# Two causal attention layers in half-height bands on TensorE, with the future zeroed after the exponential

## The chip, the core and the metric

One core of a Trainium2 chip runs the whole kernel. The metric is the device time of one execution in microseconds; lower is better. The time before is the median of three runs.

## The reference

A decoder of four blocks on x of 8 batches x 256 positions x 128 channels. Each block has self-attention, cross-attention to a context of 512 positions, and a feed-forward part, each behind a layer norm and added to x. The change touches the two causal layers of the last block, L3_attn and L3_xattn: 16 heads of 8 channels, 256 queries and 256 keys, every query seeing only keys up to its own position. L3_xattn also masks keys by batch and multiplies its result by a gate.

```python
# L3_attn
scores = jnp.einsum('bhid,bhjd->bhij', Qh, Kh) / jnp.sqrt(jnp.asarray(Dh, dtype=x.dtype))
causal = jnp.tril(jnp.ones((S, S), dtype=x.dtype))
scores = scores * causal - NEG_BIG * (1.0 - causal)
attn = jax.nn.softmax(scores, axis=-1)
vals = jnp.einsum('bhij,bhjd->bhid', attn, Vh)
...
# L3_xattn
scores = jnp.where(mask[:, None, None, :] == 0, neg_inf, scores)
future = jnp.triu(jnp.ones((Sq, Sk), dtype=bool), k=1)
scores = jnp.where(future[None, None, :, :], neg_inf, scores)
attn = jax.nn.softmax(scores, axis=-1)
attn = jnp.nan_to_num(attn, nan=0.0)
context = jnp.einsum('bhqk,bhkd->bhqd', attn, v)
gate = jax.nn.sigmoid(query @ Wg.T + bg)
output = gate * context @ Wo.T
```

## The kernel before, in words

**Order.** The layers run one after the other, with some work of the layer before (a "guest": the tail of L2_ffn in L3_attn) stepped in between. TensorE's instructions keep the order in which the program is written; on the other engines and on the queues that issue transfers, the scheduler sets the order. Every queue runs in order.

**The two causal layers** are both `_heads_attention(causal=True)`, one loop over t = 0 to 127 (batch b = t // 16, head h = t % 16) and some steps behind it. One step does:

- `maxima(t)` (line 510): the scores of head t, queries as rows, in two products of 128 and 256 keys into a PSUM tile `mh_sps` (the upper right quarter is left out); VectorE adds the causal bias, takes the maximum and stores its negative in `mh_nm` (line 523, two instructions a head).
- every fourth step, `turn` (line 544): GpSimd splits the four heads' maxima into a rounded part and the rest (`mh_hi`, `mh_nx`, lines 549 to 552); two steps later `turned` (line 554): TensorE turns them over (`mh_mps`), ScalarE copies them to `mh_m`, and one transfer that ScalarE issues (line 563) writes them into rows 96 and 97 of `q`.
- `exps(t - 12)` (line 565): first a product that writes the causal bias into the PSUM tile `mh_bsps` (256 wide in L3_attn; 384 wide in L3_xattn, with the key mask), then two products that add the scores with keys as rows. Rows 96 and 97 of `k` are ones, so the products subtract the maximum at the same time. ScalarE takes the exponential of the 384 columns (line 583, `mh_e`).
- every fourth step, `combine` (line 614) for the four heads just finished: 8 products with the values, each into a strip of 32 columns (`mh_ops`), f32 and so run in two passes, 16 in the trace. The values have a column of ones, which gives the sums. ScalarE copies the result (`mh_osb`); later `divide`, `finish`, `project_out` and `normed` end the batch.

**q and k** of the next batch are made in steps 2 to 10: TensorE projects, ScalarE adds the bias (`mh_kf`, `mh_qf`), GpSimd splits each into a rounded part and the rest (`mh_kp`, `mh_qp`, lines 428 and 429; a product of two such sums is made in one pass from four parts), and SP issues the transfers that spread heads over rows: 4 for k (line 434) and 8 for q (line 439). A head pair shares 64 rows of k: 32 rows belong to the even head and 32 to the odd one. q has one slot for each of 16 heads, with zeros in the 32 rows of the other head, so products have 96 rows (maxima) or 128 rows (exps, with the maxima's rows and zeros).

**What stands ready.** `third` (line 377), called in L2_ffn, makes a third buffer for q (four copies on ScalarE) and a transposed causal bias. `_l3_masks` (line 792), called in the middle of L3_attn, loads the key mask broadcast to 128 rows, turns it into a bias on VectorE, and gives `key_bias` (line 811), in which GpSimd adds causal and key bias with four instructions a batch.

Of the kernel before, what the change touches and what calls it, by code (L numbers as in the profile page):

```python
# [46 lines left out]
TOP = 96  # L47
FLOOR = -1.0e20
# [118 lines left out]
def _pack(inputs):  # L167
# [3 lines left out]
    for layer, mats in w.items():  # L171
# [8 lines left out]
    arrays["key_mask"] = np.ascontiguousarray(np.asarray(inputs["mask_BxS2_ik0"])[:, :S]).reshape(1, B * S)  # L180
    arrays["key_mask_t"] = np.ascontiguousarray(
        np.asarray(inputs["mask_BxS2_ik0"])[:, :S].reshape(B, 2, P).transpose(2, 0, 1)
    ).reshape(P, 2 * B)
# [161 lines left out]
class _Heads:  # L345
# [5 lines left out]
    def __init__(self, E, ctx):  # L351
# [10 lines left out]
        self.made = 0  # L362
# [14 lines left out]
    def third(self, ctx):  # L377

        pool = ctx.enter_context(self.E.tc.tile_pool(name="hd3", bufs=1, side="right"))
        q = pool.tile([P, H, S], F32R, name="mh_q2")  # L380
        for i in range(0, H, 4):
            self.E.nc.scalar.copy(
                q[:, i : i + 4, :].rearrange("p h n -> p (h n)"), self.E.plain[:, 0:1].to_broadcast([P, 4 * S])
            )
        self.q.insert(0, q)

        t = self.E.causal_t = pool.tile([P, 3, P], F32, name="causal_t")
        self.E.nc.gpsimd.memset(t, 0.0)
        for i in (0, 2):
            self.E.nc.gpsimd.affine_select(  # L390
                out=t[:, i, :], in_=t[:, i, :], compare_op=ALU.is_ge, fill=NEG, base=0,
                pattern=[[1, P]], channel_multiplier=-1,
            )

    def begin(self, layer, keys, bias=True):

        E, nc, W = self.E, self.E.nc, self.E.w(layer)
        self.layer, self.keys, self.bias = layer, keys, bias
# [11 lines left out]
    def steps(self, b):  # L410
# [29 lines left out]

        def values():
            ps = self.g.tile([P, n // P, D], F32, tag="g", name="mh_vps")
            for c in range(n // P):
                self.mm(ps[:, c, :], self.keys(b)[:, c * P : c * P + P], W("wv"), start=True, stop=True)
            to = v[:, :, : H * VW].rearrange("p k (h d) -> p k h d", d=VW)
            nc.scalar.copy(to[:, :, :, :DH], ps.rearrange("p k (h d) -> p k h d", d=DH))
# [6 lines left out]
        two = lambda f, g: lambda: (f(), g())  # L453
        spread = [lambda j=j: spread_k(j) for j in range(4)]
        spread += [lambda r=r, j=j: spread_q(r, j) for j in range(4) for r in range(2)]
        early = [lambda: project("k", self.keys(b), n), lambda: project("q", E.xt(b), S), rest]
        return early, [two(*spread[i : i + 2]) for i in range(0, 12, 2)], values
# [20 lines left out]
def _heads_attention(E, ctx, causal=False, mask=None, key_bias=None, gate=False, guest=None, known=(0,), pace=None):  # L478
# [10 lines left out]
    lag = 12 if causal else 8  # L489
# [4 lines left out]
    pe = pool("mhe", 8 if causal else 10)  # L494
# [13 lines left out]
    units, extras = {}, {}  # L508

    def maxima(t):  # L510

        b, h = divmod(t, H)
        if h == 0 and key_bias:
            extras[b] = key_bias(b)
        if h % 4 == 0:
            u = units[t // 4] = SimpleNamespace(r=ready[b], es={}, extra=extras.get(b))
            u.nm = sm.tile([P, 2, 4], F32, name="mh_nm")
        u = units[t // 4]
        q, k = u.r.q[:TOP, h, :], u.r.k[:TOP, h // 2, :]
        def lowest(at, scores, lowered):  # L520

            rest = wk.tile([P, S if causal else n], BF16, name="mh_rest")
            nc.vector.tensor_tensor_reduce(  # L523
                rest[:, : scores.shape[1]], scores, lowered, -1.0, -FLOOR, ALU.add, ALU.min, accum_out=at
            )

        col = slice(h % 4, h % 4 + 1)
        if causal:
            ps = ps_a.tile([P, 3 * P], F32, tag="a", name="mh_sps")
            mm(ps[:, :P], q[:, :P], k[:, :P], start=True, stop=True, skip_group_check=True)  # L530
            mm(ps[:, P:], q[:, P:], k, start=True, stop=True, skip_group_check=True)
            by = (u.extra or E.causal)[0].rearrange("p i k -> p (i k)")
            lowest(u.nm[:, 0, col], ps[:, :P], by[:, :P])
            lowest(u.nm[:, 1, col], ps[:, P:], by[:, P:])
            return
        for c in range(2):
            ps = ps_a.tile([P, n], F32, tag="a", name="mh_sps")
            mm(ps, q[:, c * P : c * P + P], k, start=True, stop=True, skip_group_check=True)
# [5 lines left out]
    def turn(i):  # L544

        u = units[i]
        nm = u.nm
        hi = sm.tile([P, 2, 4], F32R, name="mh_hi")
        nc.gpsimd.tensor_copy(hi, nm)  # L549
        u.nx = sm.tile([P, 2, 2, 4], F32, name="mh_nx")  # L550
        nc.gpsimd.tensor_copy(u.nx[:, :, 0, :], hi)
        nc.gpsimd.tensor_tensor(u.nx[:, :, 1, :], nm, hi, ALU.subtract)  # L552

    def turned(i):

        u = units[i]
        ps = pg.tile([P, 2, P], F32, tag="g", name="mh_mps")
        for c in range(2):
            turn_over(ps[:8, c, :], u.nx[:, c, :, :].rearrange("p a h -> p (a h)"))
        m = wk.tile([8, S], F32R, name="mh_m")  # L560
        nc.scalar.copy(m, ps[:8].rearrange("p c q -> p (c q)"))  # L561
        h0 = 4 * (i % 4)
        nc.scalar.dma_start(u.r.q[TOP : TOP + 2, h0 : h0 + 4, :].bitcast(F32), m.bitcast(F32))

    def exps(t):

        u, h = units[t // 4], t % H
        if causal:
            ps = ps_b.tile([P, 384], F32, tag="b", name="mh_bsps")
            if u.extra:  # L570
                mm(ps, E.ident16, u.extra[1], start=True, stop=False, skip_group_check=True)
            else:
                mm(
                    ps.rearrange("p (i q) -> p i q", q=P)[:, 0:3:2, :], E.later,
                    E.ident16.unsqueeze(1).to_broadcast([P, 2, P]), start=True, stop=False, skip_group_check=True,
                )
# [752 lines left out]
def _l2_ffn(E, ctx):  # L1329
# [31 lines left out]
    if E.heads:  # L1361
        E.third()
# [419 lines left out]
```

## Time and profile before

| | us |
|---|---|
| median of three runs | 1775.19 (1772.72 to 1775.53) |
| span of the profiled execution | 1770.2 |
| of it before the first scores of L3_attn | 1339 |
| L3_attn, 1339 to 1528 | 189; TensorE busy 161.4, VectorE 112.4, ScalarE 101.3, GpSimd 68.9 |
| L3_xattn, 1528 to 1707 | 179; TensorE busy 160.7, VectorE 114.2, ScalarE 97.4, GpSimd 70.9 |
| L3_ffn, from 1707 | 63 |

The profile is one execution. PE is TensorE's products, PEld its loads of the stationary operand, DVE is VectorE, ACT ScalarE, POOL GpSimd; a q behind an engine's name, or SPq, is a queue that issues transfers. A line of a window shows its start and end, its length, the busy time of each engine with the number of instructions in brackets, TensorE's granted clock, and the share and rate of the transfers. A line of a group shows the source line, engine, operation, tile written and tiles read, shapes and number, with durations as minimum, median and maximum in ns. In a timeline a line shows start and length in us and how many instructions of a kind were merged; brackets hold the idle time ahead of it and what ended it.

### The profile page before, as it was taken

The numbers are of one execution on the slowest core, as the hardware profiler recorded it, in microseconds if no ns is written. First come the engines' busy times: TensorE is split into PE (matmuls) and PEld (weight loads), VectorE is DVE, ScalarE is ACT, GpSimd is POOL, SyncE is SP. The second block draws the span as 40 slices with busy tenths as digits, with TensorE's granted clock in tenths as the row PEclk, the third lists the DMA queues.
The fourth block names the chain that finished last, engine by engine and source line by source line (L and its number), as shares of the span: only waits on it lengthen the run. The fifth ranks groups of instructions, "written<-read, shape, count | busy, mean of one in ns | idle before, by whom it ended". The sixth has DMA issues, their size and how long they took to land. (4 is left out here: it accounts for less than half of the span.)

```text
span 1770.2 us, 29308 instructions
## 1 busy us (share of the span) xinstructions
PE 1462.7 (83%) x10103; PEld 1055.3 (60%) x10141; DVE 1148.5 (65%) x3857; ACT 881.5 (50%) x1830; POOL 495.7 (28%) x987
## 2 busy tenths in 40 slices
PE   5689989999999998785578888878946799799986
PEld 3457677766665555453446666656615677677763
DVE  4567666765636676777667777767465666466756
ACT  7245455555652344325535655557644466355543
POOL 3122222221110122223433433332113433244422
PEclk9799999999999999997979999989956899899998
DMA  4011011104100000000111101111002221122100
GB/s 154 13 37 36 6 34 37 36 11 155 38 1 1 1 1 1 0 1 1 36 35 36 28 14 37 37 37 45 2 10 65 85 69 38 50 55 59 39 1 25
DMA packets 47236, 60.43 MB, mean 34 GB/s; under 512 B 5232, under 2 KB 36976, under 8 KB 46448
## 3 DMA queue, kind: packets, MB, share of 16 engines
q1 hardware_dynamic: 44720, 56.99, 11.9%
q8 instruction: 80, 1.31, 0.3%
q10 hardware_dynamic: 2368, 1.57, 0.3%
q14 instruction: 68, 0.56, 0.1%
HBM read 14.50 MB, written 1.05 MB: 9 GB/s over the span
## 5 line engine op out<-in xcount | busy, mean ns | idle before, releaser
L460 PE MATMUL mh_sps<-mh_k,mh_q 96*128 96x512 f32 (+2 forms) x1024 | 323.4, 398 | 49.0 <-DMA mh_q<-mh_qp 16.9
L460 PE MATMUL mh_bsps<-mh_q,mh_k 128*128 128x256 f32 (+1 forms) x1536 | 352.7, 335 | 7.6 <-ACT mh_e L596 4.1
L596 ACT ACTIVATE mh_e<-mh_bsps 128x512 f32<-128x512 f32 x512 | 281.0, 599 | 117.6 <-PE mh_bsps L460 110.4
L460 PEld LDWEIGHTS mh_bsps<-mh_q,mh_k 128*128 128x128 f32 x1536 | 265.8, 198 | 32.6 <-issue 6.9
L460 PEld LDWEIGHTS mh_sps<-mh_k,mh_q 96*128 96x128 f32 x1024 | 172.5, 202 | 96.2 <-issue 35.9
L523 DVE CUSTOM_DVE_ANT_0 mh_rest<-mh_sps,mask_b 128x512 bf16<-128x512 f32 x256 | 167.2, 685 | 81.4 <-PE mh_sps L460 78.4
L460 PE MATMUL mh_ops<-mh_e,mh_v 128*32 128x256 f32 (+1 forms) x3072 | 194.0, 373 | 1.3 <-DVE mh_nm L523 0.8
L542 DVE TENSOR_REDUCE mh_nm<-mh_sps 128x1 f32<-128x512 f32 x256 | 165.0, 680 | 25.7 <-PE mh_sps L460 25.2
L583 ACT ACTIVATE mh_e<-mh_bsps 128x384 f32<-128x384 f32 x256 | 118.6, 494 | 57.8 <-PE mh_bsps L460 33.5
L460 PEld LDWEIGHTS mh_ops<-mh_e,mh_v 128*32 128x32 f32 x3072 | 94.5, 111 | 66.1 <-ACT mh_e L583 5.8
L197 POOL TENSOR_SCALAR ln_rstd<-ln_mv 128x2 f32<-128x2 f32 x96 | 22.0, 229 | 386.4 <-DVE ln_mv L195 386.1
L549 POOL CAST mh_hi<-mh_nm 128x8 fp32r<-128x8 f32 x128 | 25.0, 195 | 337.9 <-DVE mh_nm L523 211.4
L523 DVE CUSTOM_DVE_ANT_0 mh_rest<-mh_sps,causal 128x128 bf16<-128x128 f32 (+1 forms) x256 | 79.4, 352 | 51.0 <-PE mh_sps L460 49.0
L523 DVE CUSTOM_DVE_ANT_0 mh_rest<-mh_sps,km_q 128x128 bf16<-128x128 f32 (+1 forms) x256 | 79.4, 350 | 43.8 <-PE mh_sps L460 42.5
L561 ACT CAST mh_m<-mh_mps 8x256 fp32r<-8x256 f32 x128 | 46.2, 361 | 102.1 <-PE mh_mps L463 100.2
L215 ACT COPY xt<-ln_ps 128x256 f32<-128x256 f32 x96 | 36.0, 375 | 120.5 <-PE ln_ps L463 62.3
L629 ACT COPY mh_osb<-mh_ops 128x256 f32<-128x256 f32 x128 | 47.7, 372 | 83.5 <-PE mh_ops L460 83.3
L886 ACT ACTIVATE moe_si<-moe_gps 128x512 f32<-128x512 f32 x64 | 38.0, 597 | 102.5 <-PE moe_gps L884 87.6
L460 PE MATMUL mh_bsps<-mask_t,ident 128*128 128x512 bf16 x219 | 84.7, 387 | 0.4 <-ACT mh_e L596 0.4
L201 DVE TENSOR_SCALAR ln_z<-x,ln_mv,ln_rstd 128x128 f32<-128x128 f32 x136 | 43.4, 360 | 54.9 <-POOL ln_rstd L198 54.7
L884 PE MATMUL moe_ups<-xt,w_L_ffn 128*128 128x512 f32 x128 | 69.2, 623 | 6.9 <-ACT moe_si L886 4.8
L463 PE MATMUL mh_mps<-ident,mh_nx 128*8 128x128 f32 x256 | 51.1, 282 | 27.7 <-POOL mh_nx L552 23.2
(360 smaller groups left out, 3086.8 us busy)
## 6 DMA issues: line engine op xcount, KB each, us to landing
mh_k<-mh_kp SPq DMA_DIRECT2D x64, 256.0 KB
mh_q<-mh_qp SPq DMA_DIRECT2D x256, 64.0 KB
mh_k<-mh_kp SPq DMA_DIRECT2D x64, 128.0 KB
w_L_ffn<-in_w_L_ffn SPq DMA_DIRECT2D x2, 1558.0 KB
w_L_attn<-in_w_L_attn SPq DMA_DIRECT2D x2, 1056.0 KB
ctx_t<-in_ctx_t SPq DMA_DIRECT2D x4, 512.0 KB
mh_q<-mh_m ACTq DMA_DIRECT2D x128, 8.0 KB
w_L_ffn<-in_w_L_ffn SPq DMA_DIRECT2D x2, 687.0 KB
```

The lines of the kernel that those rows point to most:

```text
L201: (engine or nc.vector).tensor_scalar(z[:, q, :], E.x[:, 2 * b + q, :], mv[:, q, 0:1], rstd[:, q : q + 1], ALU.subtract, ALU.mult)
L215: E.nc.scalar.copy(E.xt(b), ps.rearrange("p q t -> p (q t)"))
L460: return self.E.tc.keep_in_program_order(self.E.nc.tensor.matmul(*a, **kw))
L463: return self.E.tc.keep_in_program_order(self.E.nc.tensor.transpose(*a))
L523: nc.vector.tensor_tensor_reduce(rest[:, : scores.shape[1]], scores, lowered, -1.0, -FLOOR, ALU.add, ALU.min, accum_out=at)
L542: nc.vector.tensor_reduce(u.nm[:, c, col], ps, AX.X, ALU.max, negate=True)
L561: nc.scalar.copy(m, ps[:8].rearrange("p c q -> p (c q)"))
L583: nc.scalar.activation(e, ps, AF.Exp, scale=scale)
L596: nc.scalar.activation(e, ps, AF.Exp, scale=scale)
L629: nc.scalar.copy(osbs[b][:, u4 % 2, :], ops)
L884: nc.tensor.matmul(ps, W("w13")[:, o : o + P], xt, start=True, stop=True)
L886: nc.scalar.activation(si, pgate, AF.Silu)
```

## The change

In the causal layers even heads are put in rows 0 to 63 and odd heads in rows 64 to 127 of both q and k. In each band 32 rows hold the four parts of 8 channels, row 32 of q is ones and of k holds the key mask (or zero), the rows up to 61 are zero, and rows 62 and 63 hold the maxima in q and ones in k. Zeros and ones are written once, by 12 transfers of SP (`strips`). q needs only 8 slots for 16 heads, so that two tiles give four buffers; the third buffer is dropped. k takes 8 transfers in place of 4.

The products of `maxima(t)` and `exps(t - 13)` are written in turns, one of each; the lag is odd, so that they are of opposite bands. The bias product is dropped: the exponential is taken of all 384 columns and GpSimd then sets the future to zero in the two diagonal blocks. The key mask enters as a row of k, by two transfers a batch. `turned` comes three steps behind `turn` instead of two, its result is written by two transfers of SP instead of one of ScalarE, and `combine` comes two steps later. Ahead of the turning over and ahead of the value sums stands a filling product, a bf16 128 x 128 by 256 product into the PSUM tile that the following products overwrite.

```diff
+    def strips(self):
+        q0, q1 = self.q
+        half = H // 2
+        self.q = [q[:, at : at + half, :] for q in (q0, q1) for at in (0, half)]
+        for k in self.k:
+            self.rows(k, HIDE, LAST - HIDE, 0)
+            self.rows(k, LAST, 2, 1)
+        for q in (q0, q1):
+            self.rows(q, HIDE, 1, 1)
...
+        def strip(to, what, parts, r, j):
+            rows = slice(STRIP * r, STRIP * r + HIDE)
+            to = to[rows, :, :].bitcast(F32).rearrange("(d j) s n -> j d s n", j=4)
+            nc.sync.dma_start(to[j], got[what][64 * r : 64 * r + 64, parts[j], :])
+
+        def lower_k():
+            src = self.key_bias[b : b + 1, :]
+            for r in range(2):
+                at = STRIP * r + HIDE
+                nc.sync.dma_start(
+                    k[at : at + 1, :, :].bitcast(F32), src.unsqueeze(1).to_broadcast([1, H // 2, n])
+                )
...
+        ks = [lambda r=r, j=j: strip(k, "k", (0, 1, 0, 1), r, j) for j in range(4) for r in range(2)]
+        qs = [lambda r=r, j=j: strip(q, "q", (0, 0, 1, 1), r, j) for j in range(4) for r in range(2)]
+        if self.key_bias is not None:
+            ks.append(lower_k)
...
-    lag = 12 if causal else 8
+    lag = 13 if causal else 8
-    pe = pool("mhe", 8 if causal else 10)
+    pe = pool("mhe", 10 if causal else 10)
...
+    def warm(ps, times):
+        for _ in range(times):
+            mm(ps, E.ident16, E.causal[:, 0:2, :], **go)
...
         if causal:
+            rows = slice(STRIP * (h % 2), STRIP * (h % 2) + LAST)
+            q, k = u.r.q[rows, h // 2, :], u.r.k[rows, h // 2, :]
             ps = ps_a.tile([P, 3 * P], F32, tag="a", name="mh_sps")
-            mm(ps[:, :P], q[:, :P], k[:, :P], start=True, stop=True, skip_group_check=True)
-            mm(ps[:, P:], q[:, P:], k, start=True, stop=True, skip_group_check=True)
+            yield mm(ps[:, :P], q[:, :P], k[:, :P], **go)
+            mm(ps[:, P:], q[:, P:], k, **go)
...
     def turned(i):
+        if causal:
+            warm(ps, 1)
...
+        if causal:
+            for r in range(2):
+                at = STRIP * r + LAST
+                to = u.r.q[at : at + 2, 2 * (i % 4) : 2 * (i % 4) + 2, :]
+                nc.sync.dma_start(to.bitcast(F32), m[4 * r : 4 * r + 4, :].bitcast(F32))
+            return
         nc.scalar.dma_start(u.r.q[TOP : TOP + 2, h0 : h0 + 4, :].bitcast(F32), m.bitcast(F32))
...
     def exps(t):
-            if u.extra:
-                mm(ps, E.ident16, u.extra[1], start=True, stop=False, skip_group_check=True)
-            else:
-                mm(
-                    ps.rearrange("p (i q) -> p i q", q=P)[:, 0:3:2, :], E.later,
-                    E.ident16.unsqueeze(1).to_broadcast([P, 2, P]), start=True, stop=False, skip_group_check=True,
-                )
+            rows = slice(STRIP * (h % 2), STRIP * (h % 2) + STRIP)
+            q, k = u.r.q[rows, h // 2, :], u.r.k[rows, h // 2, :]
             for kt in range(2):
-                mm(
-                    ps[:, 256 * kt : 256 + P * kt], u.r.k[:, h // 2, kt * P : kt * P + P],
-                    u.r.q[:, h, kt * P :], start=False, stop=kt == 1, skip_group_check=True,
-                )
+                yield mm(ps[:, 256 * kt : 256 + P * kt], k[:, kt * P : kt * P + P], q[:, kt * P :], **go)
+            e = pe.tile([P, 3, P], F32, tag="e", name="mh_e")
+            flat = e.rearrange("p i q -> p (i q)")
+            nc.scalar.activation(flat, ps, AF.Exp, scale=scale)
+            own = e[:, 0:3:2, :]
+            nc.gpsimd.affine_select(
+                out=own, in_=own, compare_op=ALU.is_ge, fill=0.0, base=0, pattern=[[0, 2], [1, P]],
+                channel_multiplier=-1,
+            )
...
     def combine(i):
+        if causal:
+            warm(ops.rearrange("p (c q) -> p c q", q=P), 1)
...
+    def by_turns(s, e):
+        left = object()
+        while left is not None:
+            left = next(s, None)
+            left = next(e, None) or left
...
-        if t % 4 == 1 and 4 < t < H * B + 2:
+        if t % 4 == (2 if causal else 1) and 4 < t < H * B + 3:
             turned(t // 4 - 1)
...
-        c = t - lag - 4
+        c = t - lag - 4 - 2 * causal
```

`_l3_masks` loads the mask as 8 x 256 and makes one bias tile of it with one VectorE instruction on 8 rows; `key_bias`, `third` and the transposed bias are gone.

## The prediction

> **What bounds the kernel now.** The change touches the two causal layers alone, so I read their steady stretches first. The view of windows says how busy each engine is, and the exponentials (line 583, one for each head) say how long a batch of 16 heads takes. Each window below holds 16 of them and one cut by the edge.
>
> ```profile
> core 0: us, PE busy (x) PEld busy (x) DVE busy (x) ACT busy (x) POOL busy (x), PEclk, DMA share, GB/s
> 1447.40:1466.60 19.20, 17.93 (x182) 14.87 (x176) 11.83 (x76) 11.73 (x30) 6.81 (x21) 1.00 0.21 58
> 1581.60:1602.70 21.10, 19.06 (x183) 15.74 (x186) 13.94 (x81) 12.13 (x31) 10.06 (x26) 1.00 0.19 53
> ```
>
> ```profile
> 1447.40:1466.60 19.20, 7.29 (x17) 1.00 0.21 58
> 1581.60:1602.70 21.10, 7.49 (x17) 1.00 0.19 53
> ```
>
> A batch takes 19.2 us in L3_attn and 21.1 in L3_xattn, and TensorE is busy for 17.9 and 19.1 of it; no other engine passes 14. So TensorE sets the pace, with 1.3 and 2.0 us per batch in which it waits. What it does in one step (a head's scores for the maximum, mh_sps, and an older head's bias product and transposed scores, mh_bsps) shows in the timeline:
>
> ```profile
> 1446.14 0.10 PEld L460 LDWEIGHTS <-causal 128*128 128x128 bf16 x1
> 1446.15 0.32 PEld L460 LDWEIGHTS mh_bsps<-mh_q,mh_k 128*128 128x128 f32 x2
> 1446.39 0.30 PEld L460 LDWEIGHTS mh_sps<-mh_k,mh_q 96*128 96x128 f32 x2
> 1446.73 0.10 PEld L460 LDWEIGHTS <-causal 128*128 128x128 bf16 x1
> ...
> 1447.13 0.15 PEld L460 LDWEIGHTS mh_ops<-mh_e,mh_v 128*32 128x32 f32 x6
> ...
> 1448.40 0.19 PEld L460 LDWEIGHTS mh_vps<-w_L_attn,xt 128*128 128x128 f32 x1 [0.20 <-issue]
> ```
>
> From 1446.14 to 1446.73 is one step: 0.59 us, in which four f32 weight loads follow one another (two of 0.20 us each within 0.32, so 0.12 apart). The value sums (mh_ops) use 32-column strips: six loads are issued within 0.15 us, so loads for different strips go side by side; and on leaving that layout TensorE stands for 0.20 us.
>
> **The change part by part.** The sum is made against this execution's span, 1770.2 us; the median of the runs shown, 1775.19, is 5.0 above it.
>
> *The step.* 16 x 0.59 = 9.4 of the 17.9 us in L3_attn; the other 8.5 us stay. In L3_xattn the bias product is 384 wide instead of 256 and its mean is 335 ns against 281, so the step is 0.64, 16 of them 10.3, and 8.8 stay. The change drops the bias product and puts the two heads of a step into rows 0 to 63 and 64 to 127, in turns. No row shows two row bands at work. From below: the bands run side by side and only the two loads within a band follow each other, 2 x 0.12 = 0.24 us. From above: all four follow each other, 4 x 0.12 = 0.48. I take 0.28, since the strips of the value sums are the nearest row: 16 x 0.28 = 4.5 us a batch.
>
> *Filling products.* Eight a batch, each a bf16 load (0.10) and a 256-wide product. From below 0: it stands where TensorE would wait anyway. From above 0.28, the bias product's own length. I take 0.15: 1.2 us.
>
> *Changes of layout.* In a batch some 12 pieces of full-height work (13 with the gate) are now between steps of half height: four turns, two transposes of sums, k, q and v projections, and the end of a batch. From below each is free, as between the 96-row and 128-row products now. From above each costs what the value sums do, 0.20 out and some 0.08 in. I take half, 0.14: 1.7 and 1.8 us. The Trainium skill (TensorEngine Tiling, Key Properties) speaks against the change here: a change of tiling mode, unlike a change of tile, drains the TensorE. By that rule the 0.28 would hold and TensorE would need 1.7 us more per batch; no run here shows it for rows.
>
> TensorE then has 8.5 + 4.5 + 1.2 + 1.7 = 15.9 us a batch in L3_attn and 8.8 + 4.5 + 1.2 + 1.8 = 16.3 in L3_xattn (bounds 12.3 and 21.8).
>
> *The queue of SP.* Every transfer costs its issue:
>
> ```profile
> L434 SPq DMA_DIRECT2D mh_k<-mh_kp x16: 565/580/608, 1417.5 to 1477.2; - x16
> L439 SPq DMA_DIRECT2D mh_q<-mh_qp x31: 613/614/650, 1420.3 to 1486.4; - x31
> L563 ACTq DMA_DIRECT2D mh_q<-mh_m x16: 620/621/647, 1411.6 to 1483.8; - x16
> ```
>
> SP has 12 a batch now (4 for k, 8 for q) and ACT has 4 turns. After it k takes 8, q 8, the turns 8 on SP, and in L3_xattn the key mask 2. At 0.66 from one to the next (0.61 and the gap) that is 24 x 0.66 = 15.8 us in L3_attn and 26 x 0.66 = 17.2 in L3_xattn, from 8. ACT loses 4 x 0.62 = 2.5 us, which it had to spare. SP comes level with TensorE: this is what is late next. The second turn of a batch lies behind 8 k, 2 turns and 8 q issues that wait for POOL's split of k at about step 3; it is needed at step 17. 20 issues x 0.66 + 1.9 until it lands (ACT issued a turn at 1445.39, and SP's next issue, which waited for it, came at 1447.31) = 15.1 us for 14 steps: 17.3 us a batch, or 18.8 with the two mask transfers.
>
> *POOL.* It zeroes the future after each exponential (affine_select, 256 elements). The trace has it for 128:
>
> ```profile
> L390 POOL TENSOR_SCALAR_AFFINE_SELECT causal_t<-causal_t x2: 292/292/293, 1284.7 to 1284.9; 128x128 f32<-128x128 f32 x2
> ```
>
> A cast of 128 takes 291 ns on POOL (line 1610) and one of 256 takes 396 (line 428), so 0.40 each (from below 0.29, from above 2 x 0.29 = 0.58). 16 x 0.40 = 6.4. L3_attn: 6.8 + 6.4 = 13.2 us. L3_xattn loses the four bias instructions (0.67 + 0.43 + 0.93 + 0.60 = 2.6): 10.1 - 2.6 + 6.4 = 13.9. Both lie beside TensorE; at 0.58 they would be 16.1 and 16.8, and the cover is gone. The value sums wait for it, but are put two steps later. DVE stays at 11.8 and 14.0.
>
> *Period.* The larger of TensorE and SP, plus the waits of today: L3_attn 15.9 + 1.3 = 17.2, gain 2.0; L3_xattn 17.2 + 2.0 = 19.2, gain 1.9. Five batches of L3_attn and seven of L3_xattn run undisturbed: 5 x 2.0 + 7 x 1.9 = 23.3 us.
>
> *Mask.* Building the mask in the middle of L3_attn (four DVE instructions of 0.66 us and POOL's biases) leaves TensorE idle:
>
> ```profile
> 1388.00:1392.00 4.00, 1.05 (x6) 0.66 (x6) 3.97 (x15) 0.35 (x1) 3.92 (x8) 1.00 0.41 112
> ```
>
> 2.95 us here, and some after it: gain 4 (from 1 to 8).
>
> *Edges.* First batch of L3_attn: four more issues before its first scores, 4 x 0.66 = -2.6. The lag of 13 instead of 12 makes one paired step into two single ones in each layer: about -0.5 each, -1. The three guest-laden first batches of L3_attn: 0 to 8, I take 3. The 12 transfers that fill zeros and ones are issued before SP's wait from 1284.9 to 1328.8 us for the first k; some 12 x 0.66 = 8 us of issue hide in it. If that cover were gone they would cost those 8. The old preparation (four ACT copies, 4 us) is hidden in the quantisation as well: 0.
>
> Sum: 23.3 + 4 - 2.6 - 1 + 3 = 26.7. Span 1743.5, time **1748 us**.
>
> **Rivals.**
>
> *The bands do not run side by side* (slower). For it: nothing in the trace shows row bands, and all loads of one layout are 0.12 apart. Against it: the strips of the value sums. The step stays at 0.48 and the layout changes cost the full 0.28: TensorE 8.5 + 7.7 + 1.2 + 3.4 = 20.8 in L3_attn (+1.3 = 22.1, loss 2.9) and 21.3 in L3_xattn (23.3, loss 2.2). 5 x 2.9 + 7 x 2.2 = 30; less the 3.4 us of the other terms: 1802. It decides from where 16 steps and 12 changes together pass 17.9 - 8.5 - 1.2 = 8.2 us: with full drains from a step of 0.30 on.
>
> *SP is late* (little gained). If POOL's split of k comes one step later, 13 steps take the 15.1 us, or 16.4 with the mask transfers: 18.6 and 20.2 us a batch, gain 0.6 and 0.9. 5 x 0.6 + 7 x 0.9 = 9, with the 3.4 of the other terms 12.4: 1763; at two steps (20.1 and 21.9) it is a loss. For it: SP's 12 issues become 24, in order. Against it: the first turn of a batch and the fourth stand between projections, not behind them.
>
> *Everything at its lower bound* (faster). TensorE's 12.3 never binds, SP's 15.8 and 17.2 do, without waits: gain 3.4 and 3.9, 5 x 3.4 + 7 x 3.9 = 44, with 3.4 of the other terms 1728; with mask and guests at their best (4 and 5 more) 1719.
>
> **How the numbers follow.** Forecast 0.48 (its own range 1733 to 1762), bands not side by side 0.25, SP late 0.14, everything at its lower bound 0.13. The range must reach both the fast case and most of the slow one: 1718 to 1795; the rest of the slow case is left out. What a measurement of this kernel can tell from no change is 0.2%, 3.5 us. Faster: 0.48 + 0.13 + 0.05 of the late SP = 0.66. Same: 0.06, of SP late. Slower: 0.25 + 0.03 = 0.28.
>
> **What would show it.** The start of one pair of steps to the next some 0.3 us apart with loads of opposite bands a few ns apart (not 0.12); a batch of 16 exponentials at 17.2 and 19.2 us; SP issuing for over 80% of a batch; POOL at 13 to 14 us per batch with 0.40 for a select; no idle stretch of TensorE at the mask. A granted clock under 1.00 in the steady stretches would make all of it wrong: it is 0.77 where TensorE is busy for 15.65 of 20 us (1530 to 1550), and at 0.8 the 15.9 us become 19.9.

## The result, and the profile after

The changed kernel takes 1795.3 us (median of four runs, 1789.7 to 1803.4) against 1773.97 us: 1.012 times the kernel before, 95% interval 1.0092 to 1.0147. It is slower by 1.2%, where 1748 us was forecast. The profile is of the longest of its four executions, with a span of 1801.7 us, 31.5 more than that of before.

The windows of the changed kernel, first two batches at full clock (one of L3_attn, one of L3_xattn), then a late batch of L3_xattn; each is 16 exponentials long. Columns as before.

```profile
core 0: us, PE busy (x) PEld busy (x) DVE busy (x) ACT busy (x) POOL busy (x), PEclk, DMA share, GB/s
1458.99:1476.30 17.31, 16.68 (x170) 10.51 (x168) 11.63 (x76) 12.03 (x29) 12.77 (x37) 1.00 0.21 59
1604.72:1623.02 18.30, 17.21 (x174) 11.07 (x172) 13.99 (x81) 12.40 (x30) 13.44 (x38) 1.00 0.21 58
1683.13:1709.23 26.10, 24.36 (x165) 14.82 (x164) 14.37 (x81) 11.67 (x27) 12.43 (x38) 0.60 0.07 20
```

In these two a batch takes 17.3 and 18.3 us (18.2 and 18.9 in the two other steady batches at full clock), where 17.2 and 19.2 were forecast and 19.2 and 21.1 were needed before. The third row is the same work at a mean clock of 0.60: 26.1 us. The next view, windows of 4 us around the end of L3_attn, shows how that state comes and goes.

```profile
core 0: us, PE busy (x) PEld busy (x) DVE busy (x) ACT busy (x) POOL busy (x), PEclk, DMA share, GB/s
1496.00:1500.00 4.00, 2.46 (x30) 1.56 (x31) 1.33 (x9) 1.69 (x4) 1.65 (x7) 1.00 0.24 69
1500.00:1504.00 4.00, 4.00 (x28) 2.20 (x32) 2.48 (x15) 1.83 (x4) 1.56 (x5) 0.57 0.02 5
1504.00:1508.00 4.00, 4.00 (x32) 2.33 (x25) 1.84 (x12) 2.30 (x6) 1.51 (x5) 0.50 0.02 5
1520.00:1524.00 4.00, 4.00 (x27) 2.11 (x27) 1.29 (x8) 1.72 (x4) 1.31 (x5) 0.50 0.01 2
1524.00:1528.00 4.00, 3.94 (x27) 2.56 (x25) 0.78 (x4) 3.00 (x8) 2.77 (x6) 0.95 0.12 33
```

In the first window TensorE waits for 1.5 us (1.31 of it in one piece, at the first scores of a batch). The clock then falls to one half and stays there for 23.9 us, although the profile shows TensorE busy without a break. The records of the clock know only 1.0 and 0.5, and each stretch lasts a whole number of 3.41 us. Between the first maximum of L3_attn and the last exponential of L3_xattn the kernel before spent 43 of 361.8 us at half clock, the changed one 173 of 381.4. Two places hold the loss: counted from the first exponential of a batch to that of the next, the last two batches of L3_attn take 18.8 us more than before and the last two of L3_xattn 11.4 us more, while the other twelve together take 18.0 us less.

What TensorE waits for in these two layers (us in all, times, longest):

```profile
PE mh_sps L487 <- DMA mh_q<-mh_qp: 16.5, 8, 11.8
PE mh_sps L487 <- DVE mh_nm L546: 11.1, 10, 2.2
PE mh_sps L487 <- issue: 7.7, 8, 2.3
PE mh_bsps L487 <- DMA mh_q<-mh_m: 6.1, 1, 6.1
```

The longest, 11.8 us, is the start of L3_attn. Ten others, 0.5 to 2.3 us each, stand at the first scores of a batch, in nine of them 1.6 to 2.2 us after SP began to issue the last transfer of q; those for VectorE (`mh_nm`) stand inside batches. The 6.1 us are at the end of L3_attn. The queue of SP in one batch shows why the last q comes late:

```profile
1465.42 0.65 SPq L449 DMA_DIRECT2D mh_k<-mh_kp  x1
1466.17 1.28 SPq L605 DMA_DIRECT2D mh_q<-mh_m  x2
1467.55 4.69 SPq L449 DMA_DIRECT2D mh_k<-mh_kp  x7
1472.35 1.34 SPq L605 DMA_DIRECT2D mh_q<-mh_m  x2
1473.80 5.34 SPq L449 DMA_DIRECT2D mh_q<-mh_qp  x8
1479.24 2.71 SPq L605 DMA_DIRECT2D mh_q<-mh_m  x4
```

From the first k, which waits for GpSimd's split, to the last q SP issues almost without a pause, 13.7 us, and TensorE's next batch begins at 1480.2.

### The profile page after: what moved, and what is told of

It reads as the page before. It is cut to its first block, busy times and chain, and to the rows that moved or that the text cites. A ratio compares the mean times of both kernels' runs of the same rounds, so it can differ in the third digit from the quotient of the medians.

```text
span 1801.7 us, 29781 instructions
## 1 busy us (share of the span) xinstructions
PE 1493.3 (83%) x10013; PEld 1012.8 (56%) x10013; DVE 1147.2 (64%) x3856; ACT 882.6 (49%) x1826; POOL 572.7 (32%) x1208
## 3 DMA queue, kind: packets, MB, share of 16 engines
q8 instruction: 80, 1.31, 0.3%
## 4 chain that ended last, share of the span: by engine, by line
PE 52%; DVE 23%; POOL 11%; ACT 5%; issue 5%; DMA 3%; SPq 1%; POOLq 0%; ACTq 0%; DVEq 0%
PE mh_bsps L487 9%; PE mh_ops L487 8%; PE mh_sps L487 7%; DVE mh_nm L575 3%; POOL ln_rstd L196 2%; PE moe_dps L930 2%; DVE mh_rest L546 2%; PE moe_gps L919 2%; PE moe_ups L919 2%; PE mh_otps L490 2%; PE fa_kvps L487 2%; PE la_cps L487 2%; POOL fa_v L1172 1%; PE mh_mps L490 1%; PE mh_kps L487 1%
## 5 line engine op out<-in xcount | busy, mean ns | idle before, releaser
L487 PE MATMUL mh_sps<-mh_k,mh_q 96*128 96x512 f32 (+2 forms) x1024 | 332.0, 418 | 64.5 <-DMA mh_q<-mh_qp 24.2
L487 PE MATMUL mh_bsps<-mh_q,mh_k 128*128 128x256 f32 (+2 forms) x1536 | 356.7, 344 | 15.8 <-DMA mh_q<-mh_m 11.6
L487 PEld LDWEIGHTS mh_bsps<-mh_q,mh_k 128*128 128x128 f32 (+1 forms) x1536 | 263.9, 206 | 44.3 <-issue 19.0
L487 PEld LDWEIGHTS mh_sps<-mh_k,mh_q 96*128 96x128 f32 (+1 forms) x1024 | 175.8, 214 | 156.2 <-issue 72.6
L546 DVE CUSTOM_DVE_ANT_0 mh_rest<-mh_sps,causal 128x128 bf16<-128x128 f32 (+1 forms) x512 | 158.4, 350 | 107.1 <-PE mh_sps L487 67.5
L487 PE MATMUL mh_ops<-mh_e,mh_v 128*32 128x256 f32 (+1 forms) x3072 | 198.1, 393 | 0.3 <-DVE mh_nm L575 0.3
L623 POOL TENSOR_SCALAR_AFFINE_SELECT mh_e<-mh_e 128x256 f32<-128x256 f32 x256 | 102.3, 411 | 102.0 <-ACT mh_e L621 101.6
L487 PE MATMUL mh_bsps<-mask_t,ident 128*128 128x512 bf16 x256 | 99.4, 388 | 0.4 <-ACT mh_e L639 0.4
L930 PEld LDWEIGHTS moe_dps<-w_L_ffn,moe_act 128*128 128x128 f32 x512 | 64.7, 200 | 15.7 <-issue 8.7
```

The source lines that it names most:

```text
L487: return self.E.tc.keep_in_program_order(self.E.nc.tensor.matmul(*a, **kw))
L546: nc.vector.tensor_tensor_reduce(rest[:, : scores.shape[1]], scores, lowered, -1.0, -FLOOR, ALU.add, ALU.min, accum_out=to)
L623: nc.gpsimd.affine_select(out=own, in_=own, compare_op=ALU.is_ge, fill=0.0, base=0, pattern=[[0, 2], [1, P]], channel_multiplier=-1,)
L930: nc.tensor.matmul(ps[:, t, :], act[:, c, t * P : t * P + P], W("w2")[:, o : o + P], start=c == 0, stop=c == 1)
```

## Experiments

Theory A: half-height products fill too little of the array; once a wait has dropped the clock, they don't bring it back. Theory B: the waits on SP's transfers are the loss, and the clock only follows them. "Half clock" is the time between the two events named above, in the one profiled execution of each kernel; the changed kernel has 173 us, the kernel before 43. Every execution also has its span and its mean granted clock on record. As the clock is 1.0 or 0.5, twice the span times (1 - mean clock) is the time at half clock in the whole program: 365 to 396 us in the four executions of the changed kernel (median 388), 316 in e4, 274 to 302 in the eight of e9 and e10, and 251 to 269 (medians of the groups of runs) in the kernel before. This count serves below where one profile is too little.

| run | median us | ratio to before (95%) | half clock us | first maximum of L3_attn us |
|---|---|---|---|---|
| changed kernel | 1795.3 | 1.0120 (1.0092 to 1.0147) | 173 | 1347.8 |
| e1 no fillers | 1793.1 | 1.0126 (1.0073 to 1.0179) | 180 | 1347.1 |
| e2 fillers twice | 1787.9 | 1.0072 (1.0046 to 1.0098) | 105 | 1349.1 |
| e3 turns on ScalarE | 1862.4 | 1.0532 (1.0478 to 1.0585) | 223 | 1344.3 |
| e4 full height | 1774.6 (one run) | | 73 | 1347.5 |
| e5 full height, bias dropped | 1820.4 | 1.0283 (1.0263 to 1.0304) | 130 | 1351.9 |
| e6 late strips | 1790.0 | 1.0131 (1.0079 to 1.0183) | 151 | 1342.6 |
| e7 L3_xattn begun later | 1782.3 | 1.0063 (1.0048 to 1.0078) | 136 | 1346.0 |
| e8 lag 12 | 1805.9 (one run) | | 173 | 1345.0 |
| e9 e5 in the changed order | 1734.3 | 0.9773 (0.9758 to 0.9787) | 64 | 1340.3 |
| e10 e5, turn four steps later | 1741.8 | 0.9812 (0.9796 to 0.9829) | 74 | 1341.3 |
| e11 three mends | 1775.5 | 1.0014 (0.9986 to 1.0042) | 150 | 1343.9 |
| e12 narrow second fillers | 1793.9 | 1.0099 (1.0067 to 1.0132) | 131 | 1344.7 |

The median of the kernel before differed by up to 4 us between the groups of runs, so small differences are read from the ratios.

**e1, no fillers.**

```diff
     def turned(i):
-        if causal:
-            warm(ps, 1)
...
     def combine(i):
-        if causal:
-            warm(ops.rearrange("p (c q) -> p c q", q=P), 1)
```

> The changed kernel without its filling products (8 a batch, 128 in all); the result is the reference's. Theory A (the clock: half-height products fill too little of the array, so TensorE stays at half clock once a wait has dropped it): the time at half clock between the first maximum of L3_attn and the last exponential of L3_xattn grows from 173 us to over 210, and the layers get longer per product; the 128 x 0.195 = 25 us of fillers that go are more or less paid back, 1785 to 1805. Theory B (the waits of TensorE on SP's late transfers are the loss, the clock only follows them): time at half clock stays at 150 to 190 and the kernel is 15 to 25 us faster, 1770 to 1780.

1793.1 us, the changed kernel's time within both intervals, with 180 us at half clock instead of 173; A had named over 210. But this profile is of the shortest of e1's four executions and the changed kernel's of its longest. By mean clocks the whole program was at half clock for 408 to 485 us (median 428) without fillers and 365 to 396 (388) with them: 40 us more, as A says, if not in its size. The 25 us of products that went bought nothing; TensorE's idle time from the first exponential to the last grew by 3.4 us only (35.7 to 39.1), so they had not merely filled waits. That speaks against B.

**e2, fillers twice.**

```diff
-            warm(ps, 1)
+            warm(ps, 2)
...
-            warm(ops.rearrange("p (c q) -> p c q", q=P), 1)
+            warm(ops.rearrange("p (c q) -> p c q", q=P), 2)
```

> Each filling product of the changed kernel twice (16 a batch, 256 in all); the result is the reference's. Theory A: time at half clock falls from 173 us to under 110; at about 0.29 us lost per us at half clock (a batch of L3_xattn takes 26.1 us at half clock, 18.6 at full) that is 18 us or more back, against 128 x 0.11 to 0.195 = 14 to 25 us of products: 1780 to 1795. Theory B: time at half clock stays within 150 to 190 and the kernel is 14 to 25 us slower, 1810 to 1820.

1787.9 us with 105 us at half clock: with 128 more products the kernel is, by the ratios, 0.5% (8 us) faster than the changed one, the intervals just touching. B expected it 14 to 25 us slower. This is A, though the two profiles overstate the step: this one has the least half clock of its eight executions. By mean clocks the whole program was at half clock for 310 to 366 us (median 346) instead of 388. The expectation's price of 0.29 us took the whole batch of 26.1 us as at half clock; 21 us of it were.

**e3, turns on ScalarE.**

```diff
-                nc.sync.dma_start(to.bitcast(F32), m[4 * r
+                nc.scalar.dma_start(to.bitcast(F32), m[4 * r
```

> The changed kernel with the two transfers of each turn issued by ScalarE again instead of SP; the result is the reference's. SP has 16 issues a batch (10.6 us) instead of 24, ScalarE 8 more (5 us). Theory B: the waits of 0.5 to 2.3 us at the first scores of each batch and the 6.2 us wait at the end of L3_attn go, and with them the half clock: under 90 us of it, time 1755 to 1770. Theory A: the waits go, worth 12 to 20 us, but after any other wait the clock stays low: over 120 us at half clock, 1775 to 1785. If ScalarE becomes the bound (its batch then 11.7 + 5 of 17 us) the exponentials come late and the time is over 1790.

1862.4 us, and for neither theory's reason. It is over 1790, but TensorE waits for q (37.2 us of `mh_q<-mh_qp` in 1440 to 1700 us), not for a ScalarE that has become the bound. SP's waits in 1440 to 1560 us:

```profile
SPq L449 <- DMA mh_q<-mh_m: 31.6, 16, 3.1
```

In the trace the transfers of both queues carry eight semaphores (100 and 102 to 108), used again and again, and an issue waits for the earlier transfer with its semaphore: SP issues with 106 at 1468.12 us, 1.75 us after ScalarE did (1466.37), and with 104 at 1475.73, 1.75 us after ScalarE (1473.98). With eight of ScalarE's transfers a batch mixed into them, SP waited 16 times for a turn of ScalarE's; TensorE then waited about 5 us at the start of nearly every batch. So the changed kernel had a reason to put its turns on SP.

**e4, full height in the changed kernel.**

```diff
-            rows = slice(STRIP * (h % 2), STRIP * (h % 2) + LAST)
+            rows = slice(0, P)
...
-            rows = slice(STRIP * (h % 2), STRIP * (h % 2) + STRIP)
+            rows = slice(0, P)
...
-            nc.scalar.activation(flat, ps, AF.Exp, scale=scale)
+            nc.scalar.activation(flat, ps, AF.Exp, scale=1e-3 * scale)
```

> The changed kernel with all 128 rows in the products of maxima and exponentials, in the same order and number; each product then adds the scores of the two heads of a pair, and the exponential is taken at a thousandth of the scale, so the output is not the reference's. The transfers, waits and fillers are those of the changed kernel. Theory A: time at half clock falls from 173 us to under 70 (before: 43), while a step without neighbours takes some 0.65 us instead of 0.285. Theory B: time at half clock stays over 140 us.

73 us at half clock and 1774.6 us, 21 less than the changed kernel's median, with SP's 24 issues, the wait at the end of L3_attn (7.2 us) and longer waits at the starts of batches (1.0 to 2.3 us) all still there; from the first exponential to the last TensorE stands idle for 48.6 us here, 35.7 in the changed kernel and 42.0 in the kernel before. So the waits alone do not hold the clock down. Around one such wait (2.2 us, at the first scores of a batch) the clock drops as in the changed kernel and is back after 3.4 us:

```profile
core 0: us, PE busy (x) PEld busy (x) DVE busy (x) ACT busy (x) POOL busy (x), PEclk, DMA share, GB/s
1490.00:1494.00 4.00, 2.22 (x14) 2.24 (x14) 1.29 (x8) 1.02 (x3) 0.84 (x4) 0.82 0.11 31
1494.00:1498.00 4.00, 4.00 (x38) 3.35 (x37) 2.13 (x14) 1.93 (x5) 1.59 (x6) 0.76 0.02 4
1498.00:1502.00 4.00, 4.00 (x46) 3.47 (x46) 2.99 (x20) 2.78 (x8) 2.13 (x7) 1.00 0.02 5
```

TensorE's products in the changed kernel and in this one, for a step between two other pieces of work (start, length):

```profile
1463.82 0.60 PE L487 MATMUL mh_kps<-xt,w_L_attn 128*128 128x256 f32 x2
1464.35 0.32 PE L487 MATMUL mh_sps<-mh_k,mh_q 62*128 62x128 f32 x1
1464.35 0.38 PE L487 MATMUL mh_bsps<-mh_q,mh_k 64*128 64x256 f32 x1
1464.51 0.33 PE L487 MATMUL mh_sps<-mh_k,mh_q 62*128 62x256 f32 x1
1464.57 0.22 PE L487 MATMUL mh_bsps<-mh_q,mh_k 64*128 64x128 f32 x1
1464.77 0.28 PE L487 MATMUL mh_mps<-causal,ident 128*128 128x256 bf16 x1
```

```profile
1464.55 0.62 PE L490 MATMUL mh_otps<-ident,mh_osb 128*128 128x128 f32 x4
1464.93 0.31 PE L487 MATMUL mh_sps<-mh_k,mh_q 128*128 128x128 f32 x1
1465.07 0.33 PE L487 MATMUL mh_bsps<-mh_q,mh_k 128*128 128x256 f32 x1
1465.24 0.28 PE L487 MATMUL mh_sps<-mh_k,mh_q 128*128 128x256 f32 x1
1465.36 0.22 PE L487 MATMUL mh_bsps<-mh_q,mh_k 128*128 128x128 f32 x1
1465.42 0.28 PE L487 MATMUL mh_mps<-causal,ident 128*128 128x256 bf16 x1
```

The bands do run side by side: the two first products start together. But the step lasts until 1464.77, 0.42 us, and the full-height one 0.49 (1464.93 to 1465.42). The full-height step starts before the transposes ahead of it have ended; the half-height one starts 0.31 us after the second of the two projections (1464.04 in the trace), whose neighbours of one layout follow it in 0.22. Two half-height steps in a row are 0.285 apart, two full-height ones 0.48 to 0.51 (0.65 was expected); but only 2 or 3 of 16 steps have no other work between them. Counting each product until the next one starts, a batch of L3_attn at full clock has 16.7 us of products in the changed kernel and 16.2 here.

**e5, e9 and e10, full height with the bias dropped.** The layout, transfers and turns of the kernel before, with the changed kernel's treatment of the mask:

```diff
-            if u.extra:
-                mm(ps, E.ident16, u.extra[1], start=True, ...)
-            else:
-                mm(ps..., E.later, E.ident16..., start=True, ...)
             for kt in range(2):
-                    u.r.q[:, h, kt * P :], start=False, stop=kt == 1, ...
+                    u.r.q[:, h, kt * P :], start=True, stop=True, ...
             nc.scalar.activation(flat, ps, AF.Exp, scale=scale)
+            nc.gpsimd.affine_select(out=own, in_=own, ...)
...
+        def lower_k():
+            src = self.key_bias[b : b + 1, :]
+            nc.sync.dma_start(k[64:65, :, :].bitcast(F32), src.unsqueeze(1).to_broadcast([1, H // 2, n]))
...
-        c = t - lag - 4
+        c = t - lag - 4 - 2 * causal
```

> The kernel before with its own full-height layout (96 and 128 rows, 12 transfers of SP, turns on ScalarE, lag 12, no fillers), in which only the bias is changed as in the changed kernel: no bias product, the future zeroed by GpSimd after the exponential, the key mask as a row of k (row 64, one more transfer a batch in L3_xattn), value sums two steps later; the result is the reference's. Theory A (half height is what costs the clock; the gain lies in the bias product that goes): the clock stays full in the steady batches, at most 60 us at half clock in the two layers, a lone step takes some 0.49 us instead of 0.62 and 0.67, a batch 17.2 us in L3_attn and 18.2 in L3_xattn instead of 19.2 and 21.1, with the mask's 4 us: 1735 to 1755. Theory C (the gain of the changed kernel's full-clock batches comes from the two bands side by side): a batch stays at 18.5 us and over in both layers: 1760 to 1775.

1820.4 us, with 130 us at half clock: the expectation missed, though the step was as expected (0.49 to 0.52 in L3_attn). The trace shows two things that are new here. The ones in row 64 were written by extra copies on ScalarE, and the first maximum came at 1351.9. And GpSimd's queue: TensorE waited 4.7 us for the turn's split in each of the last six batches of L3_xattn. GpSimd at one such place:

```profile
1603.23 0.23 POOL L194 TENSOR_SCALAR ln_rstd<-ln_mv 128x2 f32<-128x2 f32 x1 [1.03 <-DVE ln_mv L192]
1603.54 0.72 POOL L195 TENSOR_TENSOR ln_rstd<-ln_rstd,neg_half 128x2 f32<-128x2 f32 x1
1604.37 1.59 POOL L198 TENSOR_SCALAR ln_z<-x,ln_mv,ln_rstd 128x128 f32<-128x128 f32 x2
1605.91 0.19 POOL L546 CAST mh_hi<-mh_nm 128x8 fp32r<-128x8 f32 x1
```

The split (the last line) is queued behind a norm, which waits for VectorE's statistics, and those for the gate's reciprocal (1.74 us). e9 takes the changed kernel's order instead, and fills q with one copy from a column that has ones in rows 64 to 95:

```diff
-    lag = 12 if causal else 8
+    lag = 13 if causal else 8
...
-        if t % 4 == 1 and 4 < t < H * B + 2:
+        if t % 4 == (2 if causal else 1) and 4 < t < H * B + 3:
```

> The full-height kernel with the bias dropped (as in the run with GpSimd's select in the layout of before), now with the changed kernel's order: lag 13, the turning over three steps after the split instead of two; and its buffers of q are filled in one copy, as in the kernel before, from a column with ones in rows 64 to 95. The result is the reference's. Theory A (full height keeps the clock, the bias product's time is the gain; what spoiled the earlier try is GpSimd's queue, in which the turn stood behind the selects and a norm, 4.7 us a batch in L3_xattn, and some 11 us of extra filling copies on ScalarE before L3_attn): the waits for mh_nx fall under 1 us a batch, first maximum of L3_attn near 1340 us, batches 17.2 to 18.0 us and 18.2 to 19.0 us, under 70 us at half clock: 1735 to 1755. If GpSimd's select costs more than the bias product gave, it stays over 1775.

1734.3 us, 0.977 of the kernel before: the fastest of all, just under the expected range, since the batches are shorter than expected. Its windows, one batch of each layer:

```profile
1454.10:1470.30 16.20, 15.55 (x163) 12.95 (x162) 11.46 (x76) 11.63 (x30) 12.84 (x36) 1.00 0.26 70
1597.60:1614.90 17.30, 16.03 (x166) 13.35 (x165) 13.71 (x81) 11.88 (x31) 13.46 (x38) 1.00 0.24 65
```

A batch takes 16.2 and 17.3 us, a us less than the batches of the changed kernel shown above, with GpSimd's work (12.8 and 13.5 us busy, the selects among it) beside TensorE. (Half height without fillers came as low in one batch of L3_attn at full clock, 16.1 us in e1.) Against the kernel before, a batch of L3_attn is 3.0 us shorter: 2.4 is TensorE's busy time (17.93 to 15.55), 0.6 its waits; in L3_xattn 3.0 of 3.8 is busy time. The new order in the kernel before, with the bias product, was not run, so its own share of the 40 us is open. The clock stays full for 89 us on end in L3_attn and for 140 in L3_xattn. e10 keeps lag 12 and turns four steps after the split:

> As the run beside it, but with lag 12 as in the kernel before and the turning over four steps after the split. Theory A: as the run beside it, 1735 to 1760; if the wait for GpSimd at the turn is given by the order of its queue and not by the number of steps, 2 to 4 us a batch of L3_xattn remain, 1760 to 1785.

1741.8 us, batches 16.7 and 17.8 us. Both orders cure the wait; e9 is a little faster. e5 differs from both in the filling copies too, and these were not run apart from the order.

**e6, late strips.** The zeros of the strips come from a tile that depends on the last batch of L2_xattn:

```diff
+        z = self.one.tile([P, P], F32, tag="z", name="nothing")
+        self.E.nc.vector.tensor_scalar(z, self.E.x[:, NT - 1, :], 0.0, None, ALU.mult)
...
-            self.rows(k, HIDE, LAST - HIDE, 0)
+            self.rows(k, HIDE, LAST - HIDE, z)
```

> The changed kernel with the zeros of k's strips copied from a tile that VectorE writes after the last batch of L2_xattn has been added to x, so that SP's 12 fills come after that batch's last turns instead of before; the result is the reference's. If the fills of 1.1 MB hold up L2_xattn's last turn (its transfer issued at 1256.4 us, PE waiting until 1262.5), then the first maximum of L3_attn comes 4 to 6 us earlier, near 1342 to 1344 us instead of 1347.8, and the kernel is 3 to 7 us faster than the changed one: 1788 to 1792. If not, it stays at 1793 to 1798.

The first maximum comes at 1342.6, 5.2 us earlier, as expected. A gain in time is not shown: the median is 5 us lower, the ratio is not; what the start gave is less than the spread that the clock makes. In the changed kernel SP issues five of the twelve fills at 1252.3 to 1259.8 us, one of the last three turns of L2_xattn is issued by ScalarE at 1256.4, and TensorE waits for it:

```profile
1262.43 1.19 PE L487 MATMUL mh_bsps<-mh_q,mh_k 128*128 128x256 f32 x4 [2.55 <-DMA mh_q<-mh_m]
```

**e7, L3_xattn begun later.**

```diff
-        if t == H * (B - 2) + 12 + free:
+        if t == H * (B - 2) + 12 + free + 4 * causal:
             E.draining()
```

> The changed kernel in which L3_xattn is begun 4 steps later in L3_attn, after the last turn of L3_attn, so that its 16 transfers of k and q stand behind the last turn's two on SP; the result is the reference's. Theory B in its narrow form (SP's order costs the 6.2 us in which TensorE waits at the end of L3_attn): that wait goes; the first maximum of L3_xattn comes at most 2 us later than with no shift, so 3 to 6 us are gained: 1789 to 1793. If the first scores of L3_xattn then wait as long for k and q, nothing is gained: 1793 to 1798.

The 6.1 us wait is gone, half clock is 136 us, and 0.57% or 10 us are gained by the ratios (13 by the medians), more than the 3 to 6 us expected. That fits a wait that costs what it is and then what the clock loses after it, but it is not clear of noise: the intervals of the two ratios leave 4.6 to 15.7 us.

**e8, lag 12.**

```diff
-    lag = 13 if causal else 8
+    lag = 12 if causal else 8
```

> The changed kernel with a lag of 12 instead of 13, so that the two heads of a step lie in the same band; the result is the reference's. If bands run side by side, a step without full-height neighbours takes 0.45 to 0.55 us instead of 0.285 at full clock, a batch at full clock 1 to 3 us more than 17.3 and 18.3, and the time is 1795 to 1825. If the order of bands does not matter, the step stays at 0.29.

1805.9 us. The two heads of one step now follow one another (products 0.17 us apart, steps in a row 0.33, where 0.45 to 0.55 was expected), but steps of opposite bands overlap instead, so that a batch at full clock still takes 17.2 to 17.8 us in L3_attn. The 10 us fall on batches at half clock (23 to 28 us); with one run, the size is uncertain.

**e11, three mends together** (e2, e6 and e7).

> The changed kernel with the three mends together: each filling product twice, the strips' fills behind L2_xattn's last turns, L3_xattn begun 4 steps later; the result is the reference's. Alone they gave 7, 5 and 13 us. If they add up (they cure the clock and two waits), 1768 to 1776, level with the kernel before; if each only cures the same half clock, 1778 to 1784. Under 100 us at half clock in the two layers.

1775.5 us over ten runs (1767.6 to 1797.9), level with the kernel before: 1.1% or 19 us less than the changed kernel by the ratios, about the sum of e2 and e7. The profile is of the longest of the ten, so its 150 us at half clock don't belong to the median; by mean clocks the whole program was at half clock for 300 to 374 us (median 335).

**e12, narrow second fillers.**

```diff
             mm(ps, E.ident16, E.causal[:, 0:2, :], **go)
+            mm(ps[:32], E.ident16[:, :32], E.causal[:, 0:2, :], **go)
```

> The changed kernel in which each filling product is followed by a second one of the same 256 columns but with a stationary operand of 32 columns instead of 128, so that it keeps TensorE streaming as long as the second filler of the doubled run but fills a quarter of the array; the result is the reference's. If the clock follows the filled share of the array, the time at half clock stays with the changed kernel's 173 us (150 to 200), and the time is that of the changed kernel or more, 1793 to 1815. If it follows how long TensorE streams at all, the time at half clock falls as in the doubled run (105 us), and the time is 1780 to 1792.

Undecided. The median of 1793.9 us is the changed kernel's, but the ratio, 1.0099, lies between the changed kernel's and e2's, and its interval overlaps both. The half clock, 131 us in one profile, lies between the two cases as well. By mean clocks the whole program was at half clock for 328 to 366 us (median 359), nearer to e2's 346 than to the changed kernel's 388, so a filler of a quarter of the array did much of what a full one did. This leans against the filled share and does not settle what the clock counts.

## Why the prediction was wrong

The step that failed is the period, "the larger of TensorE and SP, plus the waits of today": it was taken at a granted clock of 1.00, as in the windows of before. The prediction named the clock as what would break it, with one example (15.9 us become 19.9 at a clock of 0.8), but gave it no chance and no term in the sum. Over 56 steady batches of seven half-height profiles, a batch takes 17.8 us (L3_attn) or 18.4 us (L3_xattn) and 0.46 us more for each us at half clock (least squares); in the changed kernel alone the slope is 0.35 to 0.57, depending on which eight to ten batches are taken. The forecast was 29 us off the two layers (the sum without the 2.6 us at the start), 332 us; they took 381. The gap is 49 us, and 130 more us at half clock cost 60 us at 0.46 (45 to 75 by the changed kernel's slopes): enough for all of it. The 6.1 us wait and the terms of the first batches lie in the gap too, so no closer account is shown. (The profile is of the longest execution; the median lies 8 us lower.)

- **Step.** 0.28 forecast, 0.285 measured where two steps follow one another, which is so for 2 or 3 of 16. There it is right.
- **Fillers.** 0.15 forecast, 1.56 us for 8, 0.195 measured.
- **Changes of layout.** 0.14 each taken, up to 0.28 allowed. The scores take 6.6 us a batch, 2.0 over 16 x 0.285; the other products 8.5 us, against 6.4 in e4. That is 4.1 us for 13 pieces (12 were counted in L3_attn), 0.32 each: over the upper bound. The trace has it directly too: from the start of the last product ahead of a step to the start of the step 0.20 us pass in the changed kernel and 0.03 in e4, from the start of a step's last product to the next full-height one 0.20 and 0.06 (medians, 1450 to 1500 us). The rule that the prediction quoted from the Trainium skill (TensorEngine Tiling, Key Properties: changing the mode drains TensorE) fits this, and the price undoes the gain of the bands.
- **TensorE's sum.** 15.9 us in L3_attn forecast, 16.7 measured: within the bounds, but by luck, since two errors offset each other. The layout changes were 2.4 us too small, and the 8.5 us of other products that "stay" were too large: counted as the scores are here, they are 7.6 us in the kernel before and 6.4 in e4. The period of 17.3 was still as forecast, since the waits were half of the 1.3 assumed. L3_xattn was forecast at 19.2 and took 18.3 to 18.9 at full clock.
- **GpSimd.** 0.40 us a select forecast, 0.41 measured; 13.2 and 13.9 us a batch forecast, 12.8 and 13.4 measured.
- **SP.** 15.8 us a batch forecast, and it did become level with TensorE. What came late was not the second turn but the last q, at the start of the next batch. The one large wait (6.1 us at the end of L3_attn, with 16 issues of the next layer ahead of a turn) was not in the sum; the sum looked at steady batches only.
- **Mask and first batches.** 4 and 3 us forecast; the first three batches of L3_attn took 67.5 us instead of 74.9, with 6.8 us in which TensorE was idle instead of 13.9. That is near the forecast; the two terms were not taken apart.
- **The fills of the strips.** Costed at nothing, hidden in a wait of SP. The issues were hidden (17.7 us, 8 were forecast); the transfers were not: e6 shows that they put off the first maximum of L3_attn by 5 us, by way of a turn of the layer before.
- **The rival that was slower** named 1802 us, near the measured time, but for a reason (bands one after the other) that the step of 0.285 us refutes.

## What to carry to other kernels

A product of half height saves time only where many of them stand together: put between full-height work, 0.285 us became 0.42 and a change of layout on each side, and the same four products at full height were as fast. Before counting on a busy TensorE to hold its clock, look at how much of the array its products fill (173 us at half clock at half height, 73 at full height with longer waits), and price a wait there with the clock that may be lost after it. What the change wanted was in its other half: dropping the bias product and zeroing after the exponential, in the old layout and with the new order, took 40 us off the kernel before.

## What the runs showed of the hardware

In the records the clock has two states, 1.0 and 0.5, and changes only at whole steps of 3.41 us. The Trainium skill (TensorE: Matmul & The Clock Gate, What's actually happening) says so of its two states and its window, and the records agree. It speaks of how busy TensorE is; here a TensorE that the profile shows busy without a break stayed at half clock for 24 and 44 us. For ten profiles (all but e3, e5, e10 and e11, from about 1330 us to the end) I counted, in each window, the columns streamed by the products that started in it, times the share of the 128 rows and of the 128 columns in use:

| columns x share of array per 3.41 us window | at full clock: windows, then half | at half clock: windows, then full |
|---|---|---|
| under 1250 | 55, 55 | 119, 1 |
| 1250 to 2000 | 97, 45 | 268, 69 |
| 2000 to 2500 | 115, 6 | 61, 37 |
| 2500 and over | 595, 1 | 6, 6 |

This weighted count tells at full clock whether the next window stays full (96.5% of 862 windows by one threshold, 1792, fitted to the same windows); plain columns do it for 92.9%, columns by rows alone for 94.1%, and saying "full" each time for 87.6%. In the changed kernel's batches at full clock most windows have 2500 to 3500, but in its two long stretches at half clock 1536 to 2016, where the clock seldom comes back. Plain columns do not explain these stretches: among the windows at half clock between 1340 and 1700 us in which 2500 or more plain columns were streamed, 11 of 11 in e4 were followed by full clock and 8 of 29 in the changed kernel. That the array's filled share is what the clock counts is a fit over these windows; e4 and e9 (73 and 64 us at half clock) show that full height loses the clock for less time, and e12 leaves the rule itself open.
